# Attention in a convolution and mixture-of-experts kernel: one VectorE operation on both sums, a ScalarE copy, and one VectorE operation to finish

## The chip, the cores and the metric

The kernel runs on one core of one Trainium2 chip. The metric is the device time of one execution in microseconds (us); the time of a kernel is the median of several runs. The engines are called as the profile calls them: PE (TensorE, matrix products and transposes), DVE (VectorE), ACT (ScalarE), POOL (GpSimd) and SP (SyncE, here only an issuer of transfers). SBUF is the working memory of the core, PSUM the small memory that PE writes its results to.

## What is computed

Two layers follow each other. The first is a 7x7 depthwise convolution, a layer norm and a mixture of 8 experts; the second is an attention inside each token and a second mixture of experts. The change lies in the attention. There are 32 x 56 x 56 = 100,352 tokens of 128 channels, 8 heads of 16 channels. In each token and head the 16 queries meet the 16 keys of the same token:

```python
qkv = x @ w_qkv + b_qkv
q, k, v = jnp.split(qkv, 3, axis=-1)
q, k, v = (to_heads(q), to_heads(k), to_heads(v))
attn = (q * scale)[..., :, None] * k[..., None, :]
attn = jax.nn.softmax(attn, axis=-1)
out = jnp.einsum('bhlij,bhlj->bhli', attn, v)
out = out.transpose(0, 2, 1, 3).reshape(B, L, C)
return out @ w_proj + b_proj
```

For each query i there are thus two sums over 16 keys j: the sum s of exp(score), and the sum e of exp(score) times the value. The result is e / s.

## The kernel before

The kernel is a sequence of stages: the convolution, the first layer's routing and experts, the attention loop with the second layer's routing inside it (from about 4200 us to 8700 us), and the second layer's experts with the output. Only the attention loop is touched.

**Tiles, pairs and groups.** A tile is 128 tokens; there are 784. Seven tiles make a group (112 groups), which is what is loaded, normalized and projected together. Two tiles make a pair (392 pairs); the keys and values (`kv`), the bounds of the softmax (`pivots`) and the division are done for pairs. A step that takes the number `n` of a pair works on tiles n and n + 1, n even.

**The steps of a tile.** `keys` multiplies on PE; `ends` finds on DVE the largest and smallest key of each head; `pivots` makes of them on POOL the offset `c` that keeps the exponentials in bounds. `offsets` subtracts on DVE (128x2048 elements, tile `s`), `scores` multiplies by the queries on POOL (in place in `s`), `exps` takes the exponential on ACT (in place in `s`), `values` multiplies by the values on DVE (tile `ev`). `sums_s` and `sums_ev` add the 16 keys of `s` and of `ev` on PE, 16 accumulating transposes each, into the PSUM tile `sm`, which holds for a pair [channel, tile of the pair, which sum, token]: 128 x 2 x 2 x 128 numbers, one bank, two buffers. Index 0 of the third axis is the sum s, index 1 the sum e.

**The division.** `inverse_first` makes on ACT r = exp(-ln s), an approximate inverse of s. `quotients` does on DVE the rest in three operations of 128x256: d = s * r, written over s in PSUM; r = (d - 2) * r, a Newton step that leaves minus the better inverse; and oT = e * r, into the group's tile `oT` in SBUF. Where a pair straddles two groups the last of them is split into two of 128x128. The missing sign is in the projection's weights (`wp` is made with a factor of -1).

**The order.** The engines `pe`, `ve`, `sc`, `gp` are wrapped in `InOrder`, whose helper (L161) issues every instruction and binds it behind the one before it on that engine: within an engine the order is that of the text. That is why nearly every line of the profile is L161, and why instructions are told apart by their tiles. The text is a hand-written software pipeline, the loop at the end: in iteration k, step `what` with distance `back` works on tile k - back, and with `every` = 2 only on the even ones.

```python
tile_work(k, 5, inverse_first, 2)
tile_work(k, -1, ends, 2)
tile_work(k, 6, quotients, 2)
tile_work(k, 0, offsets)
tile_work(k, -1, pivots, 2)
tile_work(k, 0, scores)
tile_work(k, -2, keys, 2)
tile_work(k, 3, sums_ev)
group_work(2 * k)
tile_work(k, 1, exps)
tile_work(k, 2, values)
tile_work(k, 2, sums_s)
group_work(2 * k + 1)
```

So in an even iteration k DVE does `quotients(k-6)`, `offsets(k)`, `values(k-2)`, and in an odd one `ends(k+1)`, `offsets(k)`, `values(k-2)`. ACT does `inverse_first` in odd iterations, and in every one the first half-step of group work, `exps(k-1)`, and the second half-step. POOL does `scores` in every iteration, behind `pivots` in odd ones. PE does `keys` in even iterations, and in every one `sums_ev(k-3)` and `sums_s(k-2)` with group work behind each.

**Group work.** The two calls of `group_work` in an iteration run what the table `places` puts there: normalizing the next groups (`head_squares`, `head_scale`, `head_turn`, `head_turned`, `head_query`, `head_queries`), and projecting and routing the finished ones (`tail_sum`, `tail_summed`, `tail_row`, `tail_rows`, `tail_logits`, `tail_scale`, `tail_turn`, `tail_turned`, with `root_first` on ACT and `root_step` on POOL for the layer norms' roots). Much of it is ACT's. Each place of the table moves on by 14 half-steps, or 7 iterations, from group to group, so what meets an even or an odd iteration repeats every 14 iterations. The generator `choose` adds, for each pair of images (16 in all, about 49 tiles apart), the choice of the second layer's routing: three operations of 128x3136 on DVE (a maximum, a replacement, a masked product), an iteration of another tile lying between one and the next, two of 128x3136 on ACT, and then transposes and products on PE.

Of the kernel before, what the change touches and what calls it, by code (L numbers as in the profile page):

```python
# [8 lines left out]
F32 = mybir.dt.float32  # L9
# [3 lines left out]
ALU = mybir.AluOpType  # L13
# [4 lines left out]
P = 128  # L18
# [7 lines left out]
def conv_attn_hybrid_kernel(  # L26
# [25 lines left out]
    N, C, H, W = x.shape  # L52
# [148 lines left out]
    with tc.tile_pool(name="cv_c", bufs=1) as cc, tc.tile_pool(  # L201
        name="cv", bufs=3
# [21 lines left out]
        def products(c, part):  # L224

            bt, xi, xs = turned_bands[c % nbuf], xins[c % nbuf], sums_of_x[c]
            wide = WH + (part == 1)
            pss = [cvp.tile([P, NB, wide], F32, name="cps") for r in range(2)]
            taps = NO if part == 1 else NE
            for a in range(taps):  # L230
                for r in range(2):
                    rows = slice(r * HP, r * HP + H)
                    for b in range(2):
                        imgs = slice(b * NB, (b + 1) * NB)
                        if part < 2:
                            at_ = 2 * a + part
                            w_, m_ = at_, xi[rows, imgs, at_ : at_ + 2 * wide - 1 : 2]
                        else:
                            w_, m_ = (0, KS, KS + 1, KS + 2)[a], xs[rows, imgs, a : a + WH]
                        nc.tensor.matmul(  # L240
                            pss[r][b * HP : (b + 1) * HP], bt[rows, w_, :], m_,
                            start=(a == 0), stop=(a == taps - 1),
                            tile_position=(r * HP, b * HP), skip_group_check=True,
                        )
            return pss
# [109 lines left out]
    with tc.tile_pool(name="rt_c", bufs=1) as cc, tc.tile_pool(  # L355
        name="rt", bufs=6
# [35 lines left out]
        pe, ve, ac, gp = (InOrder(e) for e in (nc.tensor, nc.vector, nc.scalar, nc.gpsimd))  # L392
# [150 lines left out]
    with tc.tile_pool(name="sel", bufs=1) as se, tc.tile_pool(  # L543
        name="sel2", bufs=2
# [54 lines left out]
        for e in range(E):  # L599
            k = key[:, e, :]  # L600
# [181 lines left out]
    with tc.tile_pool(name="sc_c", bufs=1) as cc, tc.tile_pool(  # L782
        name="sc", bufs=4
# [50 lines left out]
        pe, ve, ac = (InOrder(e) for e in (nc.tensor, nc.vector, nc.scalar))  # L834
# [102 lines left out]
    with tc.tile_pool(name="ex_w", bufs=2) as ew, tc.tile_pool(  # L937
        name="ex", bufs=3
# [41 lines left out]
        for i, (e, b) in enumerate(blocks):  # L980
# [15 lines left out]
            xa, rows, n = got.pop(i)  # L996
# [60 lines left out]
    def fetch(i):  # L1057

        e = slice(i * Q, (i + 1) * Q)
        fw1s[i] = big.tile([C, Q, FF2], F32, name="fw1", tag="s", bufs=5)  # L1060
        nc.sync.dma_start(fw1s[i], weight1[e, :C, :].rearrange("e c f -> c e f"))
        fw2s[i] = big.tile([P, Q, NF2, C], F32, name="fw2", tag="ev", bufs=3)
        nc.sync.dma_start(fw2s[i], weight2[e, :FF2, :].rearrange("e (p f) o -> p e f o", f=NF2))

    with tc.tile_pool(name="at_c", bufs=1) as cc, tc.tile_pool(
        name="at", bufs=2
# [55 lines left out]
        pe, ve, sc, gp = (InOrder(e) for e in (nc.tensor, nc.vector, nc.scalar, nc.gpsimd))  # L1122
# [66 lines left out]
            return got  # L1189

        trs, zrs, roots, qs_, oTs, t2s, us, lgt = ({} for _ in range(8))
        kvs, pivot, ss_, evs, sms, rs = ({} for _ in range(6))


        def keys(n):
# [81 lines left out]

        def quotients(n):

            r, sm = rs.pop(n), sms.pop(n)  # L1280
            d = sm[:, :, 0, :]
            ve.tensor_tensor(d, d, r, ALU.mult)
            ve.scalar_tensor_tensor(r, d, -2.0, r, ALU.add, ALU.mult)
            (g, j), (g1, j1) = divmod(n, GJ), divmod(n + 1, GJ)
            for x, y in ((g, j), (g1, j1)):
                if y == 0:
                    oTs[x] = at.tile([C, GJ, P], F32, name="oT")
            if g == g1:
                ve.tensor_tensor(oTs[g][:, j : j + 2, :], sm[:, :, 1, :], r, ALU.mult)
            else:  # L1290
                ve.tensor_tensor(oTs[g][:, j, :], sm[:, 0, 1, :], r[:, 0], ALU.mult)
                ve.tensor_tensor(oTs[g1][:, j1, :], sm[:, 1, 1, :], r[:, 1], ALU.mult)


        def load(g):
# [273 lines left out]
        def group_work(place):  # L1569
            for what, of in work.pop(place, ()):  # L1570
                what(*of)
            if place in choices:
                choosing.append(choose(choices.pop(place)))
            if choosing and next(choosing[0], run) is run:
                choosing.pop(0)

        def tile_work(k, back, what, every=1):
            n = k - back
            if 0 <= n < NT and n % every == 0:
                what(n)  # L1580

        k = -22
        while k < NT or work or choosing or choices:
# [6 lines that stand above are left out]
            tile_work(k, -2, keys, 2)  # L1590
            tile_work(k, 3, sums_ev)
            group_work(2 * k)
            tile_work(k, 1, exps)
            tile_work(k, 2, values)
            tile_work(k, 2, sums_s)
            group_work(2 * k + 1)
            if k == NT + 4:
                for i in range(3):
                    fetch(i)
            k += 1  # L1600
# [3 lines left out]
    with tc.tile_pool(name="f_c", bufs=1) as cc, tc.tile_pool(  # L1604
        name="f", bufs=2
    ) as fp, tc.tile_pool(name="f_p", bufs=1, space=PSUM) as fps, tc.tile_pool(
        name="o", bufs=2
# [114 lines left out]
```

## Time and profile before

The median of 10 runs is 9235.56 us (9230.89 to 9238.74).

| What | Value |
|---|---|
| time of the profiled execution | 9228.17 us |
| span of that execution | 9226.1 us |
| busy in the span: PE, DVE, ACT, POOL | 8303.0, 6506.4, 5187.8, 6978.6 us |
| POOL `scores`, 128x2048, x784 | 3599.9 us, 4609 ns each |
| DVE `offsets`, 128x2048, x784 | 1788.7 us, 2282 ns each |
| DVE `values`, 128x2048, x784 | 1785.8 us, 2278 ns each |
| ACT `exps`, 128x2048, x784 | 1504.9 us, 1919 ns each |
| DVE first operation of the division, 128x256, 6000 to 7000 us | 428 ns each |
| DVE second (Newton step), 128x256, the same stretch | 425 ns each |
| DVE third, 128x256, the same stretch | 425 ns each |
| ACT logarithm of the sums, 128x256, the same stretch | 382 ns each |

Busy time is the time in which an engine works on an instruction. A line of a group of instructions reads: source line, engine, operation, what is written and what is read, shapes, how often, then the total and the mean time of one. A line of the waits reads: the engine and tile that waited, behind the arrow the engine and tile whose end released it, then the total in us, how often, and the longest. A line of the timeline reads: start in us, duration in us, engine, source line, operation, tiles, shapes, how many instructions are merged in it, and in brackets the idle time before it with its releaser. A window's line gives a stretch of the span and in it each engine's busy time with the number of its instructions, the granted clock of PE as a share of full speed, the share of the transfer engines and the GB/s that they moved. Times in windows and timelines count from the start of the span.

### The profile page before, as it was taken

How to read it: one execution, taken by the hardware profiler on the slowest of the kernel's cores; microseconds unless marked ns; L12 is line 12 of the kernel's file. 1: busy time of each engine (PE TensorE's matmuls, PEld its weight loads, DVE VectorE, ACT ScalarE, POOL GpSimd, SP SyncE). 2: the span in 40 equal slices, each digit the busy share in tenths (PEclk: the TensorE clock that was granted, in tenths of full speed). 3: DMA queues.
4: the chain of work that ended last, by engine and by line, in shares of the span. 5: the costliest groups of instructions: out<-in, count | busy, mean ns of one | idle time of the engine just before them, and what ended most of it. 6: DMA issues, size and time to landing. Idle time of an engine off the chain costs nothing. (4 is left out here: it accounts for less than half of the span.)

```text
span 9226.1 us, 156146 instructions
## 1 busy us (share of the span) xinstructions
PE 8303.0 (90%) x59112; PEld 6710.9 (73%) x59112; DVE 6506.4 (71%) x9191; ACT 5187.8 (56%) x12905; POOL 6978.6 (76%) x4879
## 2 busy tenths in 40 slices
PE   8997387776999999997999999999999999999888
PEld 3347265554666666666899999999999999999733
DVE  3349798882222222227999999999999999999623
ACT  0018443332333333335888888888888888888600
POOL 2226177777877778778999999999999999999500
PEclk9999699998999999999999999999999999999855
DMA  9996087774444444441000000000000000000299
GB/s 184 191 188 203 32 229 210 211 205 85 72 67 68 72 66 67 60 70 31 25 28 32 32 32 31 24 30 32 32 32 29 25 32 32 32 28 32 82 320 335
DMA packets 981761, 828.42 MB, mean 90 GB/s; under 512 B 517844, under 2 KB 873495, under 8 KB 961522
## 3 DMA queue, kind: packets, MB, share of 16 engines
q1 hardware_dynamic: 459410, 473.36, 18.7%
q0 software_dynamic: 177664, 188.81, 11.7%
q10 hardware_dynamic: 343936, 156.26, 6.7%
q8 instruction: 468, 7.67, 0.4%
q14 instruction: 283, 2.32, 0.1%
HBM read 465.46 MB, written 353.64 MB: 89 GB/s over the span
## 5 line engine op out<-in xcount | busy, mean ns | idle before, releaser
L161 POOL TENSOR_TENSOR s<-s,q 128x2048 f32<-128x2048 f32 x784 | 3599.9, 4609 | 75.0 <-DVE s L161 65.5
L161 ACT ACTIVATE s<-s 128x2048 f32<-128x2048 f32 x784 | 1504.9, 1919 | 684.8 <-POOL s L161 682.7
L161 POOL DMA_INDIRECT t_d<-ys,xe x992 | 1530.5, 1543 | 402.9 <-issue 229.3
L161 DVE TENSOR_TENSOR s<-kv,c 128x2048 f32<-128x2048 f32 x784 | 1788.7, 2282 | 19.7 <-POOL c L161 19.6
L161 DVE TENSOR_TENSOR ev<-s,kv 128x2048 f32<-128x2048 f32 x784 | 1785.8, 2278 | 5.5 <-ACT s L161 5.4
L161 PE MATMUL sm<-ident,ev 128*128 128x128 f32 x12544 | 1525.8, 276 | 54.2 <-DVE ev L161 54.2
L161 PE MATMUL sm<-ident,s 128*128 128x128 f32 x12544 | 1512.6, 274 | 7.6 <-ACT s L161 7.6
L161 PEld LDWEIGHTS sm<-ident,ev 128*128 128x128 f32 x12544 | 1429.9, 143 | 105.3 <-DVE ev L161 62.6
L161 PEld LDWEIGHTS sm<-ident,s 128*128 128x128 f32 x12544 | 1391.4, 142 | 20.5 <-ACT s L161 8.4
L1011 ACT ACTIVATE hT<-ph,b1t 128x512 f32<-128x512 f32 (+1 forms) x992 | 679.7, 685 | 1236.1 <-PE ph L1007 1220.5
L1022 DVE TENSOR_TENSOR ys<-py,b2t 128x512 f32<-128x512 f32 (+1 forms) x248 | 171.6, 692 | 1538.9 <-PE py L1017 1437.1
L1017 PEld LDWEIGHTS py<-w,hT 128*128 128x128 f32 x7936 | 956.6, 192 | 201.8 <-issue 91.4
L1007 PE MATMUL ph<-xeT,w 128*128 128x512 f32 (+1 forms) x1984 | 921.7, 598 | 69.6 <-DVE xeT L1003 69.6
L1017 PE MATMUL py<-w,hT 128*128 128x128 f32 x7936 | 980.7, 277 | 0.1
L820 POOL DMA_INDIRECT xb_d<-xs,rd x784 | 767.5, 979 | 240.8 <-issue 198.3
L1007 PEld LDWEIGHTS ph<-xeT,w 128*128 128x128 f32 x1984 | 348.7, 191 | 391.8 <-issue 293.7
L161 PE MATMUL pa<-rw,ct 128*128 128x256 f32 x1568 | 394.9, 394 | 125.4 <-DVE xs L161 125.4
L240 PE MATMUL cps<-xin,br 56*64 56x448 f32 (+1 forms) x3584 | 454.7, 588 | 44.6 <-ACT ea L273 30.6
L161 PE MATMUL kv<-wq,zT 128*128 128x256 f32 x1568 | 419.0, 391 | 70.6 <-DVE ev L161 70.2
L161 PEld LDWEIGHTS pa<-rw,ct 128*128 128x128 f32 x1568 | 284.3, 194 | 257.9 <-DVE xs L161 169.6
L266 POOL TENSOR_TENSOR xs<-xin 128x992 f32<-128x992 f32 x64 | 117.7, 1839 | 454.7 <-DMA xin<-in_x_dram 374.7
L161 ACT COPY add<-px 128x512 f32<-128x512 f32 x224 | 119.1, 532 | 576.3 <-PE px L161 566.8
(342 smaller groups left out, 13223.6 us busy)
## 6 DMA issues: line engine op xcount, KB each, us to landing
ct<-conv_d SPq DMA_DIRECT2D x192, 448.0 KB
xin<-in_x_dram SPq DMA_DIRECT2D x128, 392.0 KB
conv_d<-ot ACTq DMA_DIRECT2D x256, 196.0 KB
t_d<-xs ACTq DMA_DIRECT2D x112, 448.0 KB
tr<-t_d SPq DMA_DIRECT2D x112, 448.0 KB
to<-t_d SPq DMA_DIRECT2D x32, 1568.0 KB
out_dram<-oo ACTq DMA_DIRECT2D x32, 1568.0 KB
xg<-in_x_dram SPq DMA_DIRECT2D x96, 448.0 KB
```

Source lines behind the costliest of these rows:

```text
L161: r = getattr(self.engine, name)(*a, **k)
L240: nc.tensor.matmul(pss[r][b * HP : (b + 1) * HP], bt[rows, w_, :], m_, start=(a == 0), stop=(a == taps - 1), tile_position=(r * HP, b * HP ...
L266: nc.gpsimd.tensor_tensor(xs, xi[:, :, 0::2], xi[:, :, 1::2], ALU.add)
L820: s = nc.gpsimd.indirect_dma_start(out=xb_d, out_offset=bass.IndirectOffsetOnAxis(ap=idx, axis=0), in_=row, in_offset=None, bounds_check=R ...
L1007: nc.tensor.matmul(ph[:, :, :rows], w1[:, f * P : (f + 1) * P], xT[:, :, :rows], start=True, stop=True,)
L1011: nc.scalar.activation(hT[:, f, :, :rows], ph[:, :, :rows], AF.Gelu, bias=b1t[:, f : f + 1])
L1017: nc.tensor.matmul(py[:rows, j, :], hT[:, f, j, :rows], w2[:, f, :], start=(f == 0), stop=(f == NF - 1),)
L1022: nc.vector.tensor_tensor(ys[:rows], py[:rows], across(b2t, SB)[:rows], ALU.add)
```

## The change

The first operation multiplies both sums of the pair, all 128 x 512 numbers of the bank, by the approximate inverse r, in place in PSUM. It leaves d = s * r and w = e * r. A new step `products` copies w into SBUF on ACT, and a new step `corrected` finishes on DVE with (d - 2) * w, written to `oT`. The value is the same as before, since (d - 2) * r * e = (d - 2) * (r * e). `quotients` keeps its place in the loop. `products` stands behind the first half-step of group work and ahead of `exps`; `corrected` stands behind `exps` and ahead of `values`. The bank `sm` is last read by `corrected`.

```diff
-        kvs, pivot, ss_, evs, sms, rs = ({} for _ in range(6))
+        kvs, pivot, ss_, evs, sms, rs, ws = ({} for _ in range(7))
...
         def quotients(n):
 
-            r, sm = rs.pop(n), sms.pop(n)
-            d = sm[:, :, 0, :]
-            ve.tensor_tensor(d, d, r, ALU.mult)
-            ve.scalar_tensor_tensor(r, d, -2.0, r, ALU.add, ALU.mult)
+            r, sm = rs.pop(n), sms[n]
+            ve.tensor_tensor(sm, sm, r.unsqueeze(2).to_broadcast([C, 2, 2, P]), ALU.mult)
+
+        def products(n):
+
+            w = ws[n] = at.tile([C, 2, P], F32, name="w")
+            sc.copy(w, sms[n][:, :, 1, :])
+
+        def corrected(n):
+
+            sm, w = sms.pop(n), ws.pop(n)
             (g, j), (g1, j1) = divmod(n, GJ), divmod(n + 1, GJ)
             for x, y in ((g, j), (g1, j1)):
                 if y == 0:
                     oTs[x] = at.tile([C, GJ, P], F32, name="oT")
             if g == g1:
-                ve.tensor_tensor(oTs[g][:, j : j + 2, :], sm[:, :, 1, :], r, ALU.mult)
+                parts = [(oTs[g][:, j : j + 2, :], slice(0, 2))]
             else:
-                ve.tensor_tensor(oTs[g][:, j, :], sm[:, 0, 1, :], r[:, 0], ALU.mult)
-                ve.tensor_tensor(oTs[g1][:, j1, :], sm[:, 1, 1, :], r[:, 1], ALU.mult)
+                parts = [(oTs[g][:, j : j + 1, :], slice(0, 1)), (oTs[g1][:, j1 : j1 + 1, :], slice(1, 2))]
+            for to, i in parts:
+                ve.scalar_tensor_tensor(to, sm[:, i, 0, :], -2.0, w[:, i], ALU.add, ALU.mult)
...
             tile_work(k, 3, sums_ev)
             group_work(2 * k)
+            tile_work(k, 6, products, 2)
             tile_work(k, 1, exps)
+            tile_work(k, 6, corrected, 2)
             tile_work(k, 2, values)
             tile_work(k, 2, sums_s)
             group_work(2 * k + 1)
```

## The prediction

> **What bounds the kernel now.** I read the page first for the busy shares, then the windows by stage, then the waits of one stretch, then ACT, DVE and POOL side by side in time. The change touches only the attention loop, from 4219 us (first `s` of DVE) to 8673 us (last `oT`): 4450 us for 392 pairs of tiles, 11.3 us a pair. Two windows inside it (length, then busy time and instructions of PE, its weight loads, DVE, ACT and POOL, then PE's clock):
>
> ```profile
> 5000.00:6000.00 1000.00, 966.54 (x8059) 914.28 (x8058) 983.39 (x864) 838.09 (x2089) 958.34 (x556) 0.99 0.09 30
> 6000.00:7000.00 1000.00, 965.89 (x8066) 912.92 (x8064) 984.75 (x864) 831.18 (x2094) 959.91 (x554) 0.99 0.09 31
> ```
>
> DVE is the busiest with 98%, but PE and POOL stand at 96%, so the busy shares do not say who sets the pace. The waits do. From the list of waits between 5724 and 5978 us, a stretch between two routing choices (`choose`):
>
> ```profile
> ACT s L161 <- POOL s L161: 34.9, 22, 3.8
> ...
> POOL s L161 <- DVE s L161: 3.5, 1, 3.5
> ...
> DVE kx L161 <- PE kv L161: 2.4, 4, 0.7
> ...
> DVE s L161 <- POOL c L161: 0.4, 1, 0.4
> ```
>
> POOL waits for DVE once, at the very start, and then for nobody in 250 us. ACT waits for POOL 22 times, and DVE, full as it is, now and then waits for PE and POOL. So between choices POOL sets the pace: two `scores` of 4.57 us and 1.57 us of `pivots` are 10.7 us a pair, and a `root_step` of 1 us comes with each group. DVE is held a little ahead of it. Only around a choice, whose three DVE operations of 3.42 us fall into three neighbouring pairs, does POOL run dry; those places hold most of its 65.5 us of waits for DVE's `s` (49 waits, 16 choices).
>
> **What is saved.** Each pair costs DVE three operations on 128x256: 428, 425 and 425 ns in the groups of 6000 to 7000 us. From the start of the first to the start of `offsets` they take 1.26 us (6521.39 to 6522.65 below). After, the first is 128x512 over the whole of `sm`. The trace has none such. Its nearest row is `ys<-py,b2t`, also 128x512 with one operand in PSUM: 692 ns. It cannot be under 428, and twice 428, or 856, is the other end; the halves of 286 and the wholes of 425 extend to 703. I take 0.69, the nearest row. The second operation has the old 0.425. Neighbours overlap by 0.08 (2.28 long, started 2.20 apart), so 0.61 + 0.34 = 0.95: 0.31 less a pair (0.14 to 0.57 by the two ends), which would be 392 x 0.31 = 122 us if DVE alone set the time. Its busy time falls by (1.278 - 1.117) x 392 = 63 us. Pairs that straddle two groups have the last operation in two halves before and after, with the same difference.
>
> Between choices the saving is hidden behind POOL. Around a choice, where DVE sets the pace, three pairs gain 0.31 each, and 0.9 x 16 is 15 us. The most that could be gained is what POOL waits for DVE: 65.5 us, and 15 more for its other operands (3.3 us in the window of 6000 to 7000, times 4.45).
>
> The Trainium skill's Perfetto Trace Analysis, section Identifying the Most-Contended Engine, names the engine of highest occupancy as the one to optimize first. Here that is DVE, and by this rule all 122 us would be gained, for 9114. POOL's empty list of waits speaks against it.
>
> **What is added.** ACT copies 128x256 out of PSUM once a pair. Its `Ln` of the other half of the same tile takes 382 ns, so 392 x 0.38 = 149 us. As load that is covered: of 6000 to 7000 us ACT waits 149 us for POOL, and 88 copies there are 33 us. Without this cover it would cost at most the 149 us. It is the place that costs. ACT runs in text order: `exps(k-2)`, two half-steps of group work, the copy, `exps(k-1)`. DVE's second operation needs the copy and stands between `offsets(k)` and `values(k-2)`. Queued behind its wait are `values(k-2)`, `ends(k+2)` and `offsets(k+1)`, and POOL's `scores(k+1)` wait for the last. No moved step issues a DMA, so no queue of SP or POOL is passed. Now one pair, k = 408; ACT, DVE and POOL in order of time:
>
> ```profile
> 6520.87 1.94 ACT L161 ACTIVATE s<-s 128x2048 f32<-128x2048 f32 x1
> ...
> 6526.03 0.46 ACT L161 ACTIVATE st<-st 128x14 f32<-128x14 f32 x2
> 6526.40 1.91 ACT L161 ACTIVATE s<-s 128x2048 f32<-128x2048 f32 x1
> ```
>
> ```profile
> 6521.39 0.43 DVE L161 TENSOR_TENSOR sm<-sm,r 128x256 f32<-128x256 f32 x1
> ...
> 6522.65 2.28 DVE L161 TENSOR_TENSOR s<-kv,c 128x2048 f32<-128x2048 f32 x1
> 6524.85 2.28 DVE L161 TENSOR_TENSOR ev<-s,kv 128x2048 f32<-128x2048 f32 x1
> 6527.05 0.75 DVE L161 TENSOR_REDUCE kx<-kv 128x16 f32<-128x256 f32 x2
> 6527.71 2.28 DVE L161 TENSOR_TENSOR s<-kv,c 128x2048 f32<-128x2048 f32 x1
> ```
>
> ```profile
> 6520.77 9.14 POOL L161 TENSOR_TENSOR s<-s,q 128x2048 f32<-128x2048 f32 x2
> ...
> 6531.45 4.57 POOL L161 TENSOR_TENSOR s<-s,q 128x2048 f32<-128x2048 f32 x1
> ```
>
> DVE is free for the second operation at 6521.39 + 0.61 + 2.20 = 6524.20. ACT is busy with group work until 6526.44, so the copy ends at 6526.81 with 0.37 for itself and the hand-over. DVE stands for 2.6 us. Then 0.34, `values` and `ends` to the next `s` (6527.71 - 6524.85 = 2.86) and 2.28 for that `s`: it ends at 6532.3, and POOL, which started `scores(409)` at 6531.45, would start 0.9 late. Before, it had 1.5 us in hand.
>
> I did this sum for each pair that has a later tile (389). The copy comes after DVE is ready in 303, 549 us in all. Mostly DVE's lead takes it up: the next `s` is late for POOL in 72 pairs, 45 of them in the one slot of 14 (k mod 14 = 2) where `tail_rows`, `head_squares`, `tail_turned` and `root_first` meet on ACT, the rest in slots 0 and 8. The lateness sums to 64 us, and to 58 when a pair directly behind another pays only what it adds. ACT is level with POOL again between them, so each costs anew. If all hand-overs were 0.4 us quicker or slower it would be 33 or 87.
>
> **Around a choice** there is a loss too. Where DVE comes to it without its lead (1.4 us before, by the pair at tile 312), POOL runs dry earlier by up to 1.4 x 16 = 22 us. Against the 15 gained I put nothing, and keep -15 to +22.
>
> **PE** gets the bank of `sm` back later: two buffers serve, and the second operation, not the third of before, now frees one for `sums_s` of two pairs on. By the same sums it is late in 64 pairs, 94 us in all: 28 of them within the first 70 tiles, where PE runs close behind DVE, and 21 at choices that delay the operation by 3.42 us. PE has 4% of slack and DVE needs the keys behind those sums a whole tile later, so I take nothing of it; bounds are 0 and 94.
>
> Sum: 9228.2 (profiled execution) + 58 + 0 + 0 = 9286. That execution lies 7.4 us below the median of 9235.6, so 9293.
>
> **The rivals.**
> - DVE is the bound after all: 122 us would go, but POOL's waits cap it at some 80. For it: 98% busy. Against it: POOL waits for nobody between choices. 9155 to 9215 us; 0.11.
> - No measurable change (0.2%, or 18 us either way, is about what a measurement of this kernel can tell): ACT reaches the copy in time, because the hand-overs are 0.6 us quicker (21 us lost) and the choices gain 15. The place is the slot k mod 14 = 2, and the point is a shortfall under 0.5 us in it. 9217 to 9254 us; 0.16.
> - The wait costs more: PE's late banks delay the keys and so DVE, or DVE's 549 us fall through in part. 58 + 94 makes 9388, and the whole 549 less the 122 saved would be 9663. Against it: the leads counted above. 9345 and more; 0.08.
> - My forecast: ACT is late in the one slot, POOL starves there. 9254 to 9345 us by 33 to 87 with the choices' ends; 0.65.
>
> The range is 9220 to 9355 and leaves out the gains below and the tail above. Chances: faster 0.11; same 0.16; slower 0.73.
>
> **What would show it.** In the groups: `sm` 128x512 near 0.69 us, a copy `w` near 0.38 us, DVE's busy time down by 63 us. In the waits: DVE `oT` on ACT `w` with some 300 us or more, the largest of DVE in the loop; POOL's wait for DVE's `s` up from 65 to about 125 us, spread over the groups instead of sitting at the choices; ACT's for POOL down. If POOL's waits stay at 65 or fall, the lateness was absorbed and the forecast is wrong; if PE waits long for `oT` before its `sm`, the bank was the dearer part.

## The result, and the profile after

The changed kernel takes 9307.4 us (median of 8 runs, 9303.35 to 9316.3) against 9235.61 for the kernel before in the same comparison: a ratio of 1.0079, 95% interval 1.0070 to 1.0088, or 72 us more. The forecast was 9293, with 9220 to 9355. The profiled execution has a span of 9305.4 us, 79 us longer than the one before. In it the attention loop, from DVE's first `s` to the last `oT`, takes 4529.9 us; before it took 4454.0. So the loss of 76 us lies in the loop, where the change is.

The busy times on the page, and two windows of the attention loop (length, then busy time and instructions of PE, its weight loads, DVE, ACT and POOL):

```profile
PE 8332.9 (90%) x59112; PEld 6740.9 (72%) x59112; DVE 6412.6 (69%) x8799; ACT 5300.6 (57%) x13297; POOL 6981.9 (75%) x4879
```

```profile
5000.00:6000.00 1000.00, 958.36 (x7961) 905.46 (x7960) 943.45 (x763) 846.48 (x2154) 946.07 (x548) 0.98 0.09 29
6000.00:7000.00 1000.00, 953.98 (x7883) 901.25 (x7880) 946.27 (x760) 841.51 (x2112) 939.23 (x544) 0.98 0.09 30
```

DVE, 98% busy before, is 94.5% busy now. It lost 94 us of work over the span, and the kernel got slower: the saved time came back as waiting. POOL, 96% busy before, is now at 94 to 95%. Its work is the same (6978.6 and 6981.9 us), so this drop is lost time. The groups of the loop on DVE and ACT that the change touches:

```profile
L161 DVE TENSOR_TENSOR sm<-sm,r 128x512 f32<-128x512 f32 x392 | 273.3, 697 | 1.9 <-ACT r L161 1.9
L161 DVE SCALAR_TENSOR_TENSOR oT<-sm,w 128x256 f32<-128x256 f32 x336 | 141.5, 421 | 246.5 <-ACT w L161 246.0
L161 ACT COPY w<-sm 128x256 f32<-128x256 f32 x392 | 151.4, 386 | 30.3 <-DVE sm L161 29.1
```

The durations are close to those forecast, 697 for 690 ns and 386 for 380. In the last field stands what is new: DVE is idle for 246 us ahead of its second operation, until ACT's copy `w` is done. The waits of 6345 to 6576 us, again between two routing choices:

```profile
ACT s L161 <- POOL s L161: 29.5, 20, 3.2
DVE oT L161 <- ACT w L161: 16.3, 8, 3.1
...
POOL s L161 <- DVE s L161: 3.2, 5, 0.7
...
POOL kx L161 <- DVE kx L161: 1.6, 4, 0.6
```

Where POOL waited for nobody, it now waits for DVE again and again by some tenths of a microsecond. This is the pair k = 408, which the prediction worked out, in order of time on ACT, DVE and POOL:

```profile
6560.91 1.93 ACT L161 ACTIVATE s<-s 128x2048 f32<-128x2048 f32 x1
...
6566.08 0.46 ACT L161 ACTIVATE st<-st 128x14 f32<-128x14 f32 x2
6566.56 0.37 ACT L161 COPY w<-sm 128x256 f32<-128x256 f32 x1
```

```profile
6561.59 0.69 DVE L161 TENSOR_TENSOR sm<-sm,r 128x512 f32<-128x512 f32 x1
6562.19 2.28 DVE L161 TENSOR_TENSOR s<-kv,c 128x2048 f32<-128x2048 f32 x1
6566.97 0.43 DVE L161 SCALAR_TENSOR_TENSOR oT<-sm,w 128x256 f32<-128x256 f32 x1 [2.50 <-ACT w L161]
6567.31 2.28 DVE L161 TENSOR_TENSOR ev<-s,kv 128x2048 f32<-128x2048 f32 x1
6569.50 0.75 DVE L161 TENSOR_REDUCE kx<-kv 128x16 f32<-128x256 f32 x2
6570.17 2.28 DVE L161 TENSOR_TENSOR s<-kv,c 128x2048 f32<-128x2048 f32 x1
```

```profile
6570.33 0.22 POOL L161 TENSOR_TENSOR kx<-kx 128x16 f32<-128x16 f32 x1 [0.31 <-DVE kx L161]
...
6571.34 0.62 POOL L161 TENSOR_TENSOR c<-c,kx 128x256 f32<-128x256 f32 x1
6572.62 4.58 POOL L161 TENSOR_TENSOR s<-s,q 128x2048 f32<-128x2048 f32 x1 [0.67 <-PE p_q L161]
```

DVE stands for 2.50 us, until the copy is done at 6566.93. Its next `s` ends at 6572.45, and POOL, which could have started 0.31 and 0.67 us sooner, starts right after it. (The profile puts the second wait down to PE's `p_q`, which happened to end near then. `scores` reads nothing of PE; the `s` that it reads had just come from DVE.)

The idle times in brackets, added up on POOL over the loop by the tile at which they stand, show where the loss sits (us; a choice counts from 15 us ahead of its maximum to 50 us behind). A slot is the number of POOL's iteration modulo 14. What a pair of slot 2 delays is POOL's work in the next iteration, slot 3; a pair of slot 8 delays slots 9 and 10.

| POOL idle ahead of `s` and `kx` | before | after |
|---|---|---|
| first 70 tiles | 7.5 | 11.7 |
| around the 16 choices | 86.5 | 86.5 |
| everywhere else | 0.2 | 66.1 |
| of it, slots k mod 14 = 1 to 3 | 0.2 | 42.3 |
| of it, slots 9 and 10 | 0 | 23.7 |

This is 70 us more of POOL's idle time, against 72 us of the kernel's time. The list of waits by name shows less of it: the wait put down to DVE's `s`, which the prediction wanted to see at about 125 us, is 67.3 us for 65.5 before. The rest carries other names, as in the pair above (PE's `sm` 22.7 us, `p_q` 11.3, ACT's `lg` 7.3). The whole idle time ahead of `scores` is the number behind the second bar, before and after:

```profile
L161 POOL TENSOR_TENSOR s<-s,q 128x2048 f32<-128x2048 f32 x784 | 3599.9, 4609 | 75.0 <-DVE s L161 65.5
L161 POOL TENSOR_TENSOR s<-s,q 128x2048 f32<-128x2048 f32 x784 | 3599.3, 4606 | 115.3 <-DVE s L161 67.3
```

These are 40 us more; the other 29 us stand ahead of `kx`, where POOL waits 49.2 us for DVE's `kx`, for 19.8 before.

### The profile page after: what moved, and what is told of

Same layout as the page of the kernel before. It is cut to its first block, busy times and chain, and to the rows that moved or that the text cites. A ratio compares the mean times of both kernels' runs of the same rounds, so it can differ in the third digit from the quotient of the medians.

```text
span 9305.4 us, 156038 instructions
## 1 busy us (share of the span) xinstructions
PE 8332.9 (90%) x59112; PEld 6740.9 (72%) x59112; DVE 6412.6 (69%) x8799; ACT 5300.6 (57%) x13297; POOL 6981.9 (75%) x4879
## 3 DMA queue, kind: packets, MB, share of 16 engines
q0 software_dynamic: 177664, 188.81, 11.7%
## 5 line engine op out<-in xcount | busy, mean ns | idle before, releaser
L161 POOL TENSOR_TENSOR s<-s,q 128x2048 f32<-128x2048 f32 x784 | 3599.3, 4606 | 115.3 <-DVE s L161 67.3
L161 PE MATMUL sm<-ident,s 128*128 128x128 f32 x12544 | 1532.8, 276 | 94.0 <-DVE oT L161 85.2
```

The source lines that it names most:

```text
L161: r = getattr(self.engine, name)(*a, **k)
```

## The experiments

Theory A: the copy is late by its place on ACT, DVE waits, and POOL, which sets the pace between choices, starves. Rival B: the bank of the sums is freed late, and PE waits. Rival C: the copy is too much work for ACT. Times stand beside those of the kernel before on the same chip. The changed kernel was timed in another comparison, so its loop of 4529.9 us (4454.0 before) stands for it where two changed kernels are compared; the loop of each run is taken from its one profiled execution.

**The copy earlier** (label e1_copy_first):

```diff
+            tile_work(k, 6, products, 2)
             group_work(2 * k)
-            tile_work(k, 6, products, 2)
             tile_work(k, 1, exps)
```

> The changed kernel with ACT's copy ahead of the first half-step of group work instead of behind it. Theory A (the copy comes late because it stands behind two half-steps of group work; DVE waits, POOL starves in the heavy slots): in slot k mod 14 = 2 the copy comes some 2.0 us earlier (one row of 0.68, one square of 0.5, the roots' 0.8 no longer ahead of it), against a lateness at POOL of 0.6 us there, so POOL's waits outside the choices fall from 66 us to under 10 and the time to 9245 us, give or take 10. Rival B (PE gets the bank of the sums late): the bank comes earlier too, so it falls as well. Rival C (the copy's 0.38 us as load on ACT): nothing changes, 9300 to 9315.

Measured: 9215.1 us against 9240.0, ratio 0.9974 (0.9965 to 0.9983). One line of the program, moved by one place on ACT, takes off 92 us: faster than the changed kernel and than the one before. The loop takes 4435.2 us, 95 less than in the changed kernel. C, by which nothing should change, falls. The time is 20 us under the lower end of the expectation; POOL's waits at the choices fell too, from 86.5 to 67.0, which the expectation had left out. POOL's waits elsewhere are 0.8 us. The waits of 6300 to 6520 us in this kernel:

```profile
ACT s L161 <- POOL s L161: 23.1, 17, 3.2
DVE oT L161 <- ACT w L161: 7.5, 8, 1.6
...
DVE kx L161 <- PE kv L161: 1.8, 3, 0.8
```

POOL does not appear. DVE still waits for the copy, 101 us in the whole loop, but hardly anywhere long enough to pass it on to POOL. In the pair k = 408 it stands for 0.55 us, no longer 2.50. The copy can also be too early for its input: ACT waits 100.3 us here for DVE's `sm`, at no cost that shows.

**The second operation later** (label e2_after_values):

```diff
-            tile_work(k, 6, corrected, 2)
             tile_work(k, 2, values)
+            tile_work(k, 6, corrected, 2)
```

> The changed kernel with DVE's second operation behind the values instead of ahead of them; copy unmoved. Theory A: 2.2 us of DVE's wait for the copy are covered by the values, more than the 0.6 to 1.5 us by which POOL is kept waiting, so POOL's waits outside the choices fall from 66 to under 20 us and the time to 9250, give or take 12. Rival B: the bank is freed up to 2.2 us later in every pair, PE's wait for it rises from 85 us to 150 or more, and the time rises to 9330 or more. Rival C: 9300 to 9315.

Measured: 9233.9 against 9240.0, ratio 0.9994 (0.9985 to 1.0003). The loop takes 4447.5 us. POOL's waits outside the choices and the first 70 tiles are 12 us. The gain is more than A expected, once more at the choices (63.5 us). PE's waits for the bank, in the changed kernel and here:

```profile
PE sm L161 <- DVE oT L161: 85.2, 65, 3.9
```

```profile
PE sm L161 <- DVE oT L161: 126.4, 71, 4.5
```

PE waits 41 us more while the kernel gets 74 us faster (its loop 82). So PE's new wait for the bank, conspicuous as it is in the changed profile, is not what costs: B falls.

**The late bank alone** (label e3_third_late), the kernel before with its third operation in a step of its own:

```diff
             ve.scalar_tensor_tensor(r, d, -2.0, r, ALU.add, ALU.mult)
+        def corrected(n):
+            r, sm = rs.pop(n), sms.pop(n)
...
             tile_work(k, 1, exps)
+            tile_work(k, 6, corrected, 2)
             tile_work(k, 2, values)
```

> The kernel before, with only the third operation of the division moved to the place that the change gives its second: ahead of the values. No copy and no 128x512 operation; the bank of the sums is freed as late as in the change where that does not wait for ACT. Theory A: no wait on ACT, so the time of before, 9236, give or take 10. Rival B: the late bank is the cost, so most of the 72 us remain, 9280 or more. Rival C: 9236.

Measured: 9227.3 against 9240.0, ratio 0.9988 (0.9979 to 0.9997). B falls again: PE waits 43.5 us for the bank, and nothing is lost; the loop takes 4440.4 us. That it is a little faster was not expected. POOL's waits at the choices are 75.7 us, not 86.5, with all three operations still on DVE: `offsets`, which POOL waits for, now goes ahead of the third. That this order is the reason was not tested by itself.

**The load alone** (label e4_load_only), the kernel before with a copy on ACT that nobody reads:

```diff
+        def products(n):
+            sc.copy(at.tile([C, 2, P], F32, name="w"), rs.pop(n))
...
             group_work(2 * k)
+            tile_work(k, 6, products, 2)
             tile_work(k, 1, exps)
```

> The kernel before, with a copy of 128x256 on ACT at the place of the change's copy, of the inverse and into a tile that nobody reads: the load on ACT without the wait on DVE. Theory A: ACT waits for POOL longer than this in most pairs; 9236 to 9246 us. Rival B: 9236. Rival C: the load is the cost, 9290 or more.

Measured: 9240.7 against 9240.0, ratio 1.0001 (0.9992 to 1.0010). The copies took 163 us of ACT and cost nothing (loop 4455.4 us). C falls once more.

**One slot** (label e7_one_slot), the changed kernel with the copy early in one iteration of 14:

```diff
+            if k % 14 == 2:
+                tile_work(k, 6, products, 2)
             group_work(2 * k)
-            tile_work(k, 6, products, 2)
+            if k % 14 != 2:
+                tile_work(k, 6, products, 2)
```

> The changed kernel with the copy ahead of the first half-step in the iterations k mod 14 = 2 alone, one pair in seven; elsewhere it stays. Theory A (lateness slot by slot): POOL's waits in slots 2 and 3, 40 us in the changed kernel, go, and those in slots 9 and 10, 24 us, stay; the time is 9307 - 40 = 9267, give or take 12. A rival by which the wait spread over all pairs is the cost (246 us on DVE, seldom in that slot) gives a seventh of the gain: 9290 or more.

Measured: 9268.3 against 9238.3, ratio 1.0032 (1.0020 to 1.0045). Moving one copy in seven wins 39 us of the 92. POOL's waits in slots 1 to 3 fall from 42 to 4 us; those in 9 and 10 stay, 29.7 for 23.7. The lateness does add up slot by slot. That the time meets the expectation to 1 us is partly luck: POOL's waits also fell by 13 us at the choices, which was not expected, and the loop, at 4479.6 us, is 50 us shorter.

**More work on POOL** (label e8_pool_more), the kernel before:

```diff
+            gp.tensor_tensor(at.tile([P, 2, C], F32, name="more"), c, c, ALU.add)
```

> The kernel before with one more operation of 128x256 on POOL in each pair, behind the pivots, into a tile that nobody reads; its like takes 0.62 us, 243 us in all. POOL as the bound between choices (some 21 of 24.5 pairs): 0.62 to 0.7 us a pair there, 9236 + 210 to 250. Rival (DVE is the bound, POOL's 4% of idle time, 0.47 us a pair, covers most): 9236 + 80 or less.

Measured: 9446.5 against 9238.3, ratio 1.0223 (1.0208 to 1.0239), 208 us (loop 4663.6 us): most of the 240 us that the added operations took, at 612 ns each. DVE, 98% busy in the kernel before, now has to wait for POOL's pivots:

```profile
DVE s L161 <- POOL c L161: 203.6, 291, 3.3
```

In the kernel before that wait was 19.6 us. So POOL sets the pace between choices. The idle time that took up a part of the new work is that at the choices, where POOL's waits fell from 86.5 to 32.5 us.

**No copy at all** (labels e5_sbuf_late and e6_sbuf_near). The first operation writes both products to SBUF; the second reads both there, at the change's place or directly behind the first:

```diff
-            ve.tensor_tensor(sm, sm, r.unsqueeze(2).to_broadcast([C, 2, 2, P]), ALU.mult)
+            w = ws[n] = at.tile([C, 2, 2, P], F32, name="w")
+            ve.tensor_tensor(w, sm, r.unsqueeze(2).to_broadcast([C, 2, 2, P]), ALU.mult)
...
-                ve.scalar_tensor_tensor(to, sm[:, i, 0, :], -2.0, w[:, i], ALU.add, ALU.mult)
+                ve.scalar_tensor_tensor(to, w[:, i, 0, :], -2.0, w[:, i, 1, :], ALU.add, ALU.mult)
```

> No copy at all: the first operation, 128x512, writes both products to SBUF, and the second, at the change's place ahead of the values, reads them there. No wait on ACT, and the bank is free after the first operation. Theory A with POOL as the bound between choices: POOL's waits outside the choices under 3 us and at the choices at 67 or less, the time as with the early copy, 9215, give or take 10. Rival (DVE sets the pace, so that its 0.31 us a pair count in full): 9236 - 122 = 9114, and under 9180 in any case.

> As the one with no copy, and the second operation directly behind the first, where the division of before stood. POOL as the bound: 9215, give or take 10, at most 5 us from the other. Rival (the place ahead of the values is itself of use or harm, by the lead with which DVE serves POOL): 10 us or more from it.

Measured: 9548.0 and 10082.9 against 9238.3, ratios 1.0334 (1.0320 to 1.0348) and 1.0914 (1.0899 to 1.0929). All the times expected were wrong. (The second is more than 10 us from the first, as its rival had it, but not for the rival's reason.) The profile says why. DVE and POOL of the second of them, in order of time:

```profile
6502.04 0.68 DVE L161 TENSOR_TENSOR w<-sm,r 128x512 f32<-128x512 f32 x1
6502.75 3.05 DVE L161 SCALAR_TENSOR_TENSOR oT<-w 128x256 f32<-128x256 f32 x1
6505.72 2.28 DVE L161 TENSOR_TENSOR s<-kv,c 128x2048 f32<-128x2048 f32 x1
```

```profile
6500.96 4.56 POOL L161 TENSOR_TENSOR s<-s,q 128x2048 f32<-128x2048 f32 x1
6508.17 4.55 POOL L161 TENSOR_TENSOR s<-s,q 128x2048 f32<-128x2048 f32 x1 [2.65 <-ACT lg L161]
```

The operation that took 0.42 us with one input in PSUM takes 3.05 with both in SBUF, and it is shown as busy, not as waiting. It ends 0.28 us after the end of POOL's `scores` at 6505.52. So it does nearly throughout: of the 672 operations of 128x256 in the two kernels 598 start while POOL is at work, and 589 of these end 0.28 or 0.29 us behind the end of POOL's operation; the 74 that start under none take 0.41 to 0.43. In the changed kernel, with one input in PSUM, 296 of 336 start under an operation of POOL, and none takes over 0.43. The Trainium skill's SBUF — State Buffer, section SBUF: two separate sides, states this: VectorE and GpSimd share a pair of SBUF ports under a lock, and a VectorE operation with two SBUF inputs is blocked by a GpSimd operation that reads SBUF, for the whole of it, where that one started first. These two runs agree: the 128x256 operations take 1.04 us on average in the first and 2.81 in the second, for 0.42 (the halves of 128x128 take 2.77 and 1.82, for 0.29). So the copy on ACT, or rather having `d` stay in PSUM, is what keeps the change off that lock. Of the two theories these runs decide nothing, since DVE's operations are no longer what they were.

**Both moves at once** (label e10_first_and_after), the early copy and the second operation behind the values:

> Both moves at once: the copy ahead of the first half-step, the second operation behind the values. Theory A with POOL as the bound between choices: DVE's wait for the copy falls from 101 us (early copy alone) to under 30, but POOL waits outside the choices for next to nothing already, so the time stays within 10 us of the early copy alone, 9205 to 9225. Rival B in a weaker form (the bank, freed 2.2 us later again, costs something once the copy is in time): 9226 or more. Rival (DVE's wait counts wherever it stands): the 70 us saved bring 9150 or less.

Measured: 9636.3 against 9659.3, ratio 0.9978 (0.9969 to 0.9987). Both kernels are some 420 us slower on this chip. In the trace kept that lies ahead of the attention loop, which starts at 4635 us instead of 4219; the loop itself takes 4437.6 us, for 4435.2 with the early copy alone. DVE's wait for the copy is 2.5 us, and what it saved came back as other waits: 84.2 us for PE's `kv` (45.3 with the early copy alone) and 57.0 for POOL's `c` (18.3). So DVE's remaining wait there was covered by POOL. PE waits 127.5 us for the bank, and the loop is no more than 2.4 us longer for it.

## Why the prediction was right

- **POOL sets the pace between choices: right.** The added operation on POOL cost 208 of 240 us. The rule of occupancy, as the prediction applied it, gives 9114 us, or 122 us of gain. Even with DVE's wait for the copy down to 2.5 us (both moves at once) the loop was only 16 us shorter than before.
- **The copy is late by its place: right.** Early copy, late operation and the copy in one slot alone each give back POOL's waits in the slots, and some more at the choices; load and bank cost nothing.
- **The size: 58 us forecast, 70 us of POOL's idle time found.** In the pair that was worked out the sum said 2.6 us of DVE's wait and 0.9 of POOL's; the trace has 2.50 and 0.98. The slots were right too. The prediction's sum, done slot by slot over the trace of before, has 46 us for pairs of slot 2, 12 for slot 8 and 6 for slot 0 (64 in all, 58 with the correction for neighbours). Found were 37.6 us in POOL's slot 3, 12.3 in slot 9 and 4.7 in slots 1 and 2. What the sum lacked are 11.4 us in slot 10: behind a pair of slot 8 POOL waits once more, ahead of the `scores` after next, and the sum looked at the next one alone. Behind a pair of slot 2 it has no such wait. There POOL does a `root_step` of 1 us between the two `scores`, which probably covers it.
- **DVE's wait: too high.** 549 us in 303 pairs were added up against the clock of before; 246 us in 145 pairs were found. A DVE that has just waited comes later to the next pair and waits less there: in slots 4 and 10, right behind 2 and 8, the same sum has 67 and 60 us, and 3 were found in each. DVE's `s` there ends 0.9 and 0.3 us ahead of POOL's `scores` on average, before 1.9 and 1.1. The 300 us or more that the prediction wanted to see as a sign were not there, and the theory held without them.
- **DVE's busy time: 63 us less forecast, 94 found.** The sum of durations left out the overlap. Of the three operations of before only the last overlaps its neighbour (in the pair k = 408 it runs from 6522.31 to 6522.73 us, and `offsets` starts at 6522.65); of the two that are left each does, by 0.08 us or so. Nothing follows from it for the time.
- **The choices: nothing, right as a sum.** POOL's waits there are the same to a tenth (86.5 us before and after); that gain and lost lead cancelled so exactly is luck. The early copy, which keeps the lead, gets 19.5 us there, against the 15 forecast for the gain alone. The run with the third operation late got 11 there, with all three operations still in place, so not all of it is due to two operations in place of three.
- **The bank: nothing, right.** PE's wait for it came, 85 us against a bound of 94, and no price of it was found: with 126 us of it the kernel was faster.

## What to carry to other kernels

Where several engines are 94 to 98% busy, look for the one that never waits before crediting an operation taken off the busiest. A helper operation moved to an idle engine is not free because that engine has time: it is ready when its queue lets it be, so put it as far ahead in that queue as its own inputs allow, and behind it on the other engine put first what a third engine waits for. If an operation on VectorE is rewritten, keep one of its two tensors in PSUM as long as GpSimd is at work in SBUF.

## What the runs showed that was not expected

A VectorE operation of 128x256 with both inputs in SBUF took 2.81 us on average beside GpSimd's 4.6 us operations, for 0.42 with one input in PSUM, and the profile counts all of it as busy: DVE reads 99.7% of 5000 to 8000 us in that kernel, and by an estimate from the mean durations some 975 us of the loop's 5299 are time that DVE stood behind GpSimd. And an order alone counts: the third operation of the division moved behind `offsets` and ahead of `values`, with nothing else changed, made the kernel before 0.12% faster (0.03 to 0.21), about half of what the early copy gained on it.
